# Layer 1 of a four-layer graph network: one 128-row product, or two 64-row products in two PSUM banks

## The chip, the cores and the metric

The kernel runs on one core of a Trainium2 chip. The time is device microseconds of one execution; for the kernel before it is the median of three runs. The profile is of one more execution, taken by the hardware profiler. The engines are PE (TensorE; PEld is its weight load), DVE (VectorE), ACT (ScalarE), POOL (GpSimd) and SP (SyncE, which issues DMAs). PSUM is the memory that PE writes its products to, in banks of 512 float32 columns on 128 partitions.

## The reference

A graph has 6250 nodes with 128 features and 206250 edges, sorted by destination. Four layers follow each other. Each normalises `x`, takes the part above zero as `h`, gathers `h` over the edges and adds its output to `x`:

```python
edge_index = jnp.stack([src, dst])
h = jnp.maximum(_layernorm(x), 0.0)
x = x + layer0(h, edge_weight, src, dst)   # weighted sums over edges, two linear maps, leaky relu
h = jnp.maximum(_layernorm(x), 0.0)
x = x + layer1(h, edge_index)              # mean over edges, see below
h = jnp.maximum(_layernorm(x), 0.0)
x = x + layer2(h, x_clique, edge_index)    # mean of x_clique rows over edges, one linear map
h = jnp.maximum(_layernorm(x), 0.0)
x = x + layer3(h, edge_index)              # sums over edges, a gated unit, one linear map

def layer1(x, edge_index):
    src, dst = edge_index
    deg = segment_sum(ones, dst, num_segments=n)
    agg = segment_sum(x[src], dst, num_segments=n) / jnp.maximum(deg, 1.0)[:, None]
    f = gelu(agg @ Wl.T + bl + x @ Wr.T, approximate=False)
    ...                                    # normalised over all nodes, plus x
```

## The kernel before

The nodes lie in 49 blocks of 128. The first part (function `strip`, lines L620 to L916) goes over 25 strips of two blocks of destination nodes. It turns the edges into one-hot matrices, and products of 64 rows each (`count`, L754) make from them, for a strip, a matrix of edge counts and one of edge weights, source by destination. Layer 0 runs in the same part: `layer0` (L791) multiplies `h0` with the weights matrix `edge_w` of the strip before, in float32. A float32 product takes two instructions on PE. Each block of 128 source nodes is taken there as two products of 64 rows, into two banks of the tile `pL`; ACT copies one bank (L796) and DVE adds the other (L797). `finish0` follows with full-height products of 128 rows (L825, L826, L846) and 64-row transposes (L809). The counts are written to DRAM (`cnt_d`) as one byte each.

Layers 1 to 3 then use the counts as a dense matrix. The function `dense` (L935) goes over 13 chunks of destination nodes, in `CHUNKS`: 11 of four blocks (512 columns), one of three (384) and one of two (256). For a chunk it accumulates, over all 49 blocks of source nodes, into one PSUM tile `acc` of two buffers. The features are held as two parts whose sum is `h` (`parts`, type fp32r), so each source block needs two products, j = 0 and 1: 98 products per chunk, 1274 per layer. This is L992. The right-hand side is a block of the counts, widened from bytes to fp32r.

A chunk is cut into 10 steps of up to five source blocks. For a step, `bring` fetches the bytes by DMA from SP's queue (tile `ring`, one fetch for two steps) and widens them into one of three buffers `wide`: in layer 1, where `seen` is given and each widening also counts the edges, three or two blocks by DVE (L973) and two or three by ACT (L975). `bring` for step n + 1 stands in the program ahead of the products of step n. All of this is under a hand-written schedule (`manual_schedule`): each engine executes its instructions in the order of the program text.

Work behind a chunk is a generator, `end1` for layer 1. `run` calls it when the chunk's last products have been issued. Its first piece, `copied` (L1114), brings the sum from `acc` to the SBUF tile `wa` with an ACT copy (L1116). Its later pieces run one by one between the steps that follow (`between`): `times` (L1123, four full-height float32 products with the weights `wl`), the scaling on DVE (L1131), the gelu on ACT (L1137), sums over nodes on POOL (L1020), and a subtraction (L1145). Also put between the steps of layer 1 are products for the inverse degrees (L1075), for a first mean (L1029) and for the last clique row (L1156). `end2` and `end3` use `copied` too.

[...] `pB` and `pM` are used by `end2` and `end3` (L1233, L1237, L1254, L1265), not by `end1`.

Of the kernel before, what the change touches and what calls it, by code (L numbers as in the profile page):

```python
# [9 lines left out]
F32 = mybir.dt.float32  # L10
# [6 lines left out]
P = 128  # L17
# [457 lines left out]
CB = 4  # L475
# [23 lines left out]
def fast(ctx: ExitStack, tc: tile.TileContext, a: dict, out: bass.AP, flag: bass.AP):  # L499


    nc = tc.nc
# [47 lines left out]
    def flat(t):  # L550
        return t.rearrange("p b f -> p (b f)")
# [47 lines left out]
    with ExitStack() as bx:  # L599
# [6 lines left out]
        psum = bx.enter_context(tc.tile_pool(name="b_psum", bufs=1, space=bass.MemoryType.PSUM))  # L606
# [304 lines left out]
        end = ends.pop()  # L911
# [21 lines left out]
    psum = ctx.enter_context(tc.tile_pool(name="f_psum", bufs=1, space=bass.MemoryType.PSUM))  # L933

    def dense(parts, by_node, seen=None, ahead=None):  # L935


        last = NB if by_node else NQB
        held = []

        def bring(c, g, nb, q):

            now = wide.tile([P, KP, CB * P], F32R, name="wide")
            if not by_node:
                t = ring.tile([P, KQ, CB // 2 * P], U16, name="ring")
                n = -(-nb // 2) * P
                nc.sync.dma_start(t[:, :, :n], cntT_d[:, q : q + KQ, g // 2 * P : g // 2 * P + n])
                t = flat(t).bitcast(U8).rearrange("p (k r n e) -> p k r e n", k=KQ, n=P, e=2)
                for eng, k in ((nc.vector.tensor_copy, slice(0, 3)), (nc.scalar.copy, slice(3, 5))):
                    if nb == 1:  # L950
                        eng(now[:, k, :P], t[:, k, 0, 0])
                    else:
                        eng(now[:, k, : 2 * n].rearrange("p k (r e n) -> p e k r n", e=2, n=P),  # L953
                            t[:, k, : n // P].rearrange("p k r e n -> p e k r n"))
                return [(q + k, now[:, k, : nb * P]) for k in range(KQ)]
            e = q % 2
            if e == 0:
                if ahead and c == 0:
                    ahead(q + 2 * KP)
                t = ring.tile([P, CB, KP * P], U16, name="ring")  # L960
                nc.sync.dma_start(t[:, :nb], cnt_d[c, :, :nb, q // 2 * P : (q // 2 + KP) * P])
                held[:] = [flat(t).bitcast(U8).rearrange("p (b k n e) -> p e k b n", b=CB, k=KP, e=2)[:, :, :, :nb]]
            to = now[:, :, : nb * P].rearrange("p k (b n) -> p k b n", n=P)
            of = held[0][:, e]
            ks = min(KP, (NB - q + 1) // 2)
            if seen is None:
                nc.vector.tensor_copy(*(v[:, :3].rearrange("p k b n -> p b k n") for v in (to, of)))  # L967
                nc.scalar.copy(to[:, 3:ks], of[:, 3:ks])  # L968
            for k in range(ks if seen is not None else 0):
                s = q + 2 * k  # L970
                total = seen[:, c, s : s + 1]
                if k < 3 - e:
                    nc.vector.tensor_scalar(to[:, k], of[:, k], 1.0, None, op0=ALU.mult, op1=ALU.add, accum_out=total)  # L973
                else:
                    nc.scalar.activation(to[:, k], of[:, k], AF.Copy, accum_out=total)  # L975
            return [(q + 2 * k, now[:, k, : nb * P]) for k in range(ks)]

        chunks = [(c, *CHUNKS[c]) for c in ORDER] if by_node else [(c, *at) for c, at in enumerate(CHUNKS2)]
        end = NB - 2 if by_node else NQB - 1
        parts_of = [q + e for q in range(0, NB, 2 * KP) for e in range(2)] if by_node else range(0, NQB, KQ)  # L980
        steps = [(c, g, nb, q) for c, g, nb in chunks for q in parts_of]
        ready = bring(*steps[0])
        yield
        for n, (c, g, nb, q) in enumerate(steps):
            now = ready
            if n + 1 < len(steps):
                ready = bring(*steps[n + 1])
            if q == 0:
                acc = psum.tile([P, CB * P], F32, name="acc", bufs=2)
            for s, rhs in now:  # L990
                for j in range(2):
                    nc.tensor.matmul(acc[:, : nb * P], parts[:, s, j, :], rhs,  # L992
                                     start=s + j == 0, stop=s == end and j == 1)
            yield (g, nb, acc) if q == parts_of[-1] else None

    running, waiting = [], []
# [116 lines left out]

    def copied(acc, w):  # L1114
        agg = work.tile([P, CB * P], F32, name="wa", bufs=5)
        nc.scalar.copy(agg[:, :w], acc[:, :w])  # L1116
        return agg

    def times(agg, weight, nb):
# [6 lines left out]
    def end1(g, nb, acc):  # L1126
        agg = copied(acc, nb * P)
        yield
        pa = times(agg, wl, nb)
        for j in range(nb):  # L1130
            nc.vector.scalar_tensor_tensor(f[:, g + j, :], pa[:, j * D : (j + 1) * D],  # L1131
                                           inv1[:, g + j : g + j + 1], f[:, g + j, :],
                                           op0=ALU.mult, op1=ALU.add)
        yield
        fb = f[:, g : g + nb, :]
        fg = flat(fb)
        nc.scalar.activation(fg, fg, AF.Gelu)  # L1137
        over_nodes(f_sum, fb, g, nb)
        yield
        if g == 0:  # L1140
            yield
            p = over_all(fb, nb)
            nc.vector.scalar_tensor_tensor(first, p, 1.0 / (nb * P), mean_scale, op0=ALU.mult, op1=ALU.mult)
            yield
        nc.vector.tensor_sub(fb, fb, bcast(first, nb))  # L1145
        yield
        sq = work.tile([P, GB, D], F32, name="wb", bufs=3)
        nc.scalar.activation(sq[:, :nb, :], fb, AF.Square)
        over_nodes(sq_sum, sq, g, nb)
# [44 lines left out]
    def end2(g, nb, acc):  # L1194
        w = nb * P
        cols = slice(g * P, g * P + w)
        agg = copied(acc, w)
        yield
        pa = times(agg, wc, nb)
# [47 lines left out]
    def end3(g, nb, acc):  # L1247
        w = nb * P
        cols = slice(g * P, g * P + w)
        agg = copied(acc, w)  # L1250
        yield
        gates, r_z = [], ("pA", "pM")
# [41 lines left out]
    with tc.manual_schedule():  # L1294
# [18 lines left out]
        chores[11 * n1].append(lambda: nc.vector.tensor_add(b_rz, b_ih[:, :2], b_hh[:, :2]))  # L1313
        chores[11 * n1 + 3].append(lambda: nc.vector.tensor_add(b_res, gn_bias, bc))
        run(dense(h_parts, True, deg2, h_up_to), end1, chores)
        running.extend(waiting)
        running.append(graph_norm())
        waiting.clear()

        layer2 = dense(q_parts, False)  # L1320
        next(layer2)
        normed = running[-1]
        for done in layer2:
            between(normed not in running)
            if done:
                work_2 = end2(*done)
                next(work_2)
                waiting.append(work_2)
        layer3 = dense(m_parts, True)
        next(layer3)  # L1330

# [67 lines left out]
```

## Time and profile before

| what | value |
| --- | --- |
| median of three runs | 1887.61 us (1885.89 to 1888.15) |
| profiled execution, its own time | 1886.66 us |
| its span, first to last instruction | 1884.5 us |
| granted PE clock, mean | 0.988 |
| PE busy | 1783.6 us, 95% |
| DVE busy | 1397.3 us, 74% |
| ACT busy | 1204.7 us, 64% |
| POOL busy | 463.1 us, 25% |
| DMA, mean | 123 GB/s |

Layer 0 and the counting take the span up to about 1028 us, layer 1 from there to 1327, layer 2 to about 1507 and layer 3 the rest.

In the lines of the profile, a group has line, engine, operation, output<-inputs, shape and count, then busy time and the mean ns of one instruction, then the idle time of the engine ahead of it and what ended it. In a shape such as `64*128 64x256`, the first pair is the rows and columns of PE's array that a product takes, and the second the rows and columns that are streamed. A row of a timeline has the start, the length from the first start to the last end, and the number of like instructions that were merged into it. The profile marks fp32r products as f32. Ends of products are modelled; starts are recorded.

### The profile page before, as it was taken

To read this page: it belongs to the slowest core of one execution; us is meant where nothing else is said; L and a number is where in the kernel's file an instruction comes from. 1 tells how busy PE (TensorE), PEld (TensorE's weight loads), DVE (VectorE), ACT (ScalarE), POOL (GpSimd) and SP (SyncE) were. 2 spreads that over 40 slices of the span, in tenths; PEclk is the share of its full clock that TensorE was granted. 3 is DMA by queue.
4 is the path that set the end of the run, shared out by engine and by line. 5 is a ranking of instruction groups with operands and counts; after the bars stand their busy time and mean duration, and the time that the engine had idled before them with its cause. 6 is when DMAs were issued, how large, how long until landed. Compare 5 with 4: busy or idle time off the path is not lost. (4 is left out here: it accounts for less than half of the span.)

```text
span 1884.5 us, 65347 instructions
## 1 busy us (share of the span) xinstructions
PE 1783.6 (95%) x28188; PEld 1504.1 (80%) x28188; DVE 1397.3 (74%) x2952; ACT 1204.7 (64%) x2834; POOL 463.1 (25%) x429
## 2 busy tenths in 40 slices
PE   0799999999999999999997999999999999999997
PEld 0688888888888888888886788888888877787775
DVE  5888888888888888888873877777787845444543
ACT  2877777777777777777772677777565654444442
POOL 3224333433334323433321111111132200000000
PEclk9799999999999999999998999999999999999998
DMA  3235555554645554554212555554554544344431
GB/s 76 80 89 130 116 131 114 122 125 115 122 101 135 106 130 109 118 123 112 71 58 95 180 178 163 167 158 124 148 151 142 159 128 139 119 143 133 148 116 52
DMA packets 262350, 231.98 MB, mean 123 GB/s; under 512 B 101553, under 2 KB 246052, under 8 KB 262052
## 3 DMA queue, kind: packets, MB, share of 16 engines
q1 hardware_dynamic: 252243, 210.20, 41.4%
q0 software_dynamic: 8944, 17.12, 3.2%
q8 instruction: 223, 3.65, 0.8%
q10 hardware_dynamic: 864, 0.39, 0.2%
q14 instruction: 76, 0.61, 0.1%
HBM read 130.50 MB, written 76.67 MB: 110 GB/s over the span
## 5 line engine op out<-in xcount | busy, mean ns | idle before, releaser
L791 PE MATMUL pL<-edge_w,h 64*128 64x256 f32 (+1 forms) x4900 | 616.5, 386 | 5.0 <-DVE agg L797 1.0
L992 PE MATMUL acc<-wide,parts 128*128 128x512 f32 (+2 forms) x2548 | 578.8, 386 | 12.8 <-DVE wide L973 9.4
L992 PEld LDWEIGHTS acc<-wide,parts 128*128 128x128 f32 x2548 | 463.9, 190 | 112.8 <-issue 14.5
L763 ACT CAST cnt<-pK 128x400 uint8<-128x400 f32 x784 | 396.6, 506 | 197.8 <-PE pK L754 181.7
L791 PEld LDWEIGHTS pL<-edge_w,h 64*128 64x128 f32 x4900 | 433.9, 187 | 46.3 <-DVE agg L797 6.7
L754 PEld LDWEIGHTS <-s_hot 64*128 64x128 bf16 x18816 | 371.7, 95 | 69.9 <-issue 18.5
L754 PE MATMUL pK<-k_hot,s_hot 64*128 64x49 bf16 (+1 forms) x18816 | 389.0, 193 | 21.6 <-ACT edge_w L761 11.9
L761 ACT COPY edge_w<-pK 128x392 f32<-128x392 f32 x784 | 399.5, 510 | 0.0
L735 DVE TENSOR_TENSOR k_hot<-k_hot,by_edge 128x2352 bf16<-128x2352 bf16 x196 | 272.8, 1392 | 8.0
L732 DVE TENSOR_TENSOR s_hot<-iota,keys 128x2048 bf16<-128x2048 bf16 x196 | 240.0, 1224 | 41.2 <-PE pK L754 37.9
L973 DVE TENSOR_SCALAR_CACHE_REDUCE wide<-ring 128x512 fp32r<-128x512 uint8 (+2 forms) x325 | 193.2, 650 | 27.6 <-issue 15.3
L975 ACT ACTIVATE wide<-ring 128x512 fp32r<-128x512 uint8 (+2 forms) x312 | 184.8, 595 | 38.9 <-ACT wide L975 19.9
L642 POOL DMA_INDIRECT dst<-in_dst,off_i x50 | 83.4, 1668 | 401.2 <-DVE node L680 394.4
L968 ACT CAST wide<-ring 128x1024 fp32r<-128x1024 uint8 (+3 forms) x130 | 120.8, 957 | 77.0 <-PE acc L992 66.7
L967 DVE CAST wide<-ring 128x1536 fp32r<-128x1536 uint8 (+2 forms) x130 | 118.9, 938 | 58.6 <-PE acc L992 41.5
L992 PE MATMUL acc<-wide,q_parts 128*128 128x512 f32 (+2 forms) x650 | 157.4, 392 | 1.2 <-DVE wide L953 1.2
L992 PEld LDWEIGHTS acc<-wide,q_parts 128*128 128x128 f32 x650 | 115.7, 189 | 28.1 <-DVE wide L953 3.1
L734 DVE TENSOR_TENSOR k_hot<-iota,keys 128x800 bf16<-128x800 bf16 x196 | 126.4, 645 | 0.0
L1288 POOL DMA_DIRECT2D out<-x x12 | 10.0, 837 | 320.9 <-DVE x L1286 290.9
L1267 DVE SCALAR_TENSOR_TENSOR wb<-pT,f_b_hh,wb 128x512 f32<-128x512 f32 (+2 forms) x13 | 9.4, 720 | 97.2 <-PE pT L1264 90.7
L642 POOL DMA_INDIRECT src<-in_src,off_i x50 | 76.4, 1527 | 15.2 <-issue 14.6
L1116 ACT COPY wa<-acc 128x512 f32<-128x512 f32 (+2 forms) x39 | 21.8, 560 | 82.6 <-PE acc L992 82.6
(181 smaller groups left out, 1564.6 us busy)
## 6 DMA issues: line engine op xcount, KB each, us to landing
ring<-cnt_d SPq DMA_DIRECT2D x110, 640.0 KB, 4.4
cnt_d<-cnt SPq DMA_DIRECT2D x49, 800.0 KB, 4.1
cntT_d<-tt SPq DMA_DIRECT2D x125, 160.0 KB, 2.0
ring<-cntT_d SPq DMA_DIRECT2D x60, 320.0 KB, 3.2
ring<-cnt_d SPq DMA_DIRECT2D x10, 480.0 KB, 3.7
ring<-cnt_d SPq DMA_DIRECT2D x10, 320.0 KB, 3.0
xs<-in_x SPq DMA_DIRECT2D x12, 256.0 KB, 3.0
xs<-in_x SPq DMA_DIRECT2D x24, 128.0 KB, 3.8
```

Source lines behind the costliest of these rows:

```text
L642: nc.gpsimd.indirect_dma_start(out=t, out_offset=None, in_=col[name], in_offset=bass.IndirectOffsetOnAxis(ap=idx, axis=0))
L732: nc.vector.tensor_tensor(s_hot, count_up(P), at(0, P), op=ALU.is_equal)
L734: nc.vector.tensor_tensor(k_hot[:, :, 0], count_up(NBP), at(1, NBP), op=ALU.is_equal)
L735: nc.vector.tensor_tensor(k_hot[:, :, 1:, :NB], k_hot[:, :, :1, :NB].to_broadcast([P, tq, 3, NB, TI]), parts.to_broadcast([P, tq, 3, NB, T ...
L754: nc.tensor.matmul(pk[:, h, to], s_hot[r, u, :, t], rhs, start=j == 0, stop=True, skip_group_check=True)
L761: nc.scalar.copy(m.rearrange("p b (i h) -> p b i h", h=WN), by_block[:, 1, :NB])
L763: nc.scalar.copy(m.rearrange("p b e (i h) -> p b e i h", h=WN), by_block[:, 0].rearrange("p (b e) i h -> p b e i h", e=2))
L791: nc.tensor.matmul(pl[:, h, :w], h0[r, s, :], edge_w[r, s, :w], start=s == 0, stop=s == NB - 1)
L968: nc.scalar.copy(to[:, 3:ks], of[:, 3:ks])
L973: nc.vector.tensor_scalar(to[:, k], of[:, k], 1.0, None, op0=ALU.mult, op1=ALU.add, accum_out=total)
L975: nc.scalar.activation(to[:, k], of[:, k], AF.Copy, accum_out=total)
L992: nc.tensor.matmul(acc[:, : nb * P], parts[:, s, j, :], rhs, start=s + j == 0, stop=s == end and j == 1)
```

## The change

In layer 1 alone (`seen` is given there and nowhere else), a chunk gets a second PSUM tile of 512 columns, `pB` and `pM` in turn. Each product of 128 source nodes becomes two: the first 64 nodes into `acc`, the last 64 into the second tile, one directly behind the other. `copied` copies the first tile with ACT as before, and DVE then adds the second one to the copy. In layers 2 and 3 `acc` is a list of one tile, and the products are those of before.

```diff
             if q == 0:
-                acc = psum.tile([P, CB * P], F32, name="acc", bufs=2)
+                acc = [psum.tile([P, CB * P], F32, name="acc", bufs=2)]
+                if seen is not None:
+                    acc.append(psum.tile([P, CB * P], F32, name=("pB", "pM")[n // len(parts_of) % 2]))
             for s, rhs in now:
                 for j in range(2):
-                    nc.tensor.matmul(acc[:, : nb * P], parts[:, s, j, :], rhs,
-                                     start=s + j == 0, stop=s == end and j == 1)
+                    for i, t in enumerate(acc):
+                        r = slice(i * P // len(acc), (i + 1) * P // len(acc))
+                        nc.tensor.matmul(t[:, : nb * P], parts[r, s, j, :], rhs[r],
+                                         start=s + j == 0, stop=s == end and j == 1)
             yield (g, nb, acc) if q == parts_of[-1] else None
...
     def copied(acc, w):
         agg = work.tile([P, CB * P], F32, name="wa", bufs=5)
-        nc.scalar.copy(agg[:, :w], acc[:, :w])
+        nc.scalar.copy(agg[:, :w], acc[0][:, :w])
+        if len(acc) > 1:
+            nc.vector.tensor_add(agg[:, :w], agg[:, :w], acc[1][:, :w])
         return agg
```

## Prediction

> **What bounds the kernel now.** I read the page first. Its slices show the TensorE (PE) busy at nine tenths nearly throughout, and its groups put layers 1 and 3 (line L992, `parts`) at the largest cost but one:
>
> ```profile
> L791 PE MATMUL pL<-edge_w,h 64*128 64x256 f32 (+1 forms) x4900 | 616.5, 386 | 5.0 <-DVE agg L797 1.0
> L992 PE MATMUL acc<-wide,parts 128*128 128x512 f32 (+2 forms) x2548 | 578.8, 386 | 12.8 <-DVE wide L973 9.4
> ```
>
> L791 is layer 0, which already works in halves of 64 rows. Then I cut the span at the layers with the table by windows. Layer 1 runs from 1029 to 1327 us:
>
> ```profile
> 1028.00:1327.00 299.00, 292.22 (x1389) 244.51 (x1390) 225.71 (x737) 211.81 (x664) 50.07 (x55) 0.99 0.54 164
> 1100.00:1150.00 50.00, 50.00 (x230) 41.60 (x229) 37.83 (x121) 36.66 (x112) 9.26 (x9) 1.00 0.59 178
> ```
>
> The columns are length, then busy time of PE, its weight loads, DVE, ACT and POOL. Once the layer has started (from about 1053 us), PE has next to no idle time up to its last, narrow chunk. So what a product costs on PE goes straight into the time, and DVE (38 of 50 us) matters only where PE must wait for it.
>
> The PE timeline gives the pace; the first two rows are from a view of a whole chunk, the last two from views cut inside a chunk:
>
> ```profile
> 1113.63 1.05 PE L1123 MATMUL pA<-f_WlT,wa 128*128 128x128 f32 x8
> 1114.44 22.50 PE L992 MATMUL acc<-wide,parts 128*128 128x512 f32 x98
> ...
> 1119.78 10.59 PE L992 MATMUL acc<-wide,parts 128*128 128x512 f32 x46
> ...
> 1162.69 10.58 PE L992 MATMUL acc<-wide,parts 128*128 128x384 f32 x60
> ```
>
> A row runs from its first start to its last end. 46 products in 10.59 us, less one duration of 0.39, over 45 steps, make 0.227 us each; with 384 columns (10.58 - 0.34) / 59 = 0.1736. The 53 ns between them for 128 columns are 0.415 ns per column; 512 columns make 0.212, so 14 ns of the 227 depend on no column. Only these 14 ns can be saved by any arrangement that streams the same columns. The whole chunk's row, 22.50 - 0.39 over 97 steps, holds 0.09 more than 97 x 0.227: its first product takes longer.
>
> **The pairs.** The change replaces each of layer 1's 1274 products (98 steps in 13 chunks) by two with 64 rows each and all of its columns (512 in 1078 of them), into two banks. Work streamed per row of the array is the same; so nothing is gained unless part of the 14 ns goes. The trace shows such pairs in layer 0, from the PE timeline:
>
> ```profile
> 990.50 12.34 PE L791 MATMUL pL<-edge_w,h 64*128 64x256 f32 x112
> ...
> 1004.22 0.94 PE L791 MATMUL pL<-edge_w,h 64*128 64x128 f32 x12
> ...
> 1005.11 0.89 PE L791 MATMUL pL<-edge_w,h 64*128 64x128 f32 x12
> 1005.93 0.49 PE L825 MATMUL po<-f_W1T,agg 128*128 128x128 f32 x2
> 1006.25 0.39 PE L826 MATMUL po<-f_W2T,inter 128*128 128x128 f32 x2
> 1006.48 0.39 PE L825 MATMUL po<-f_W1T,agg 128*128 128x128 f32 x2
> 1006.70 0.39 PE L826 MATMUL po<-f_W2T,inter 128*128 128x128 f32 x2
> 1007.02 2.95 PE L791 MATMUL pL<-edge_w,h 64*128 64x128 f32 x48
> ```
>
> 112 products are 56 pairs, two starts some 0.01 apart: (12.34 - 0.38 - 0.01) / 55 = 0.217 us a pair with a longer first one in it, 0.216 without. One such product takes 0.377 by itself, so two in 0.216 do run at once, with two weight loads. Half against whole shows at 128 columns: 24 pairs in 2.95, less 0.27 for the last, 0.01 and 0.08 for the longer first, over 23, are 0.1126; eight full-height products in L1123's 1.05, less 0.275, over 7, are 0.111. So halves are 1 to 2 ns dearer than the whole in f32, and not cheaper. For layer 1's number type (fp32r, half the cycles per column) no 64-row pair is in this trace. Bounds: down to 0.216 (the f32 pair, which streams as long) saves 1274 x 11 ns = 14 us; both fixed parts in a row, 0.227 + 0.014 = 0.241, costs 18 us; no overlap at all, 2 x 0.227, costs 289 us. I take the nearest comparison, half against whole in one type: +1 ns, 1.3 us, with 0 to 2.5 as its range.
>
> [...]
>
> **Switching between halves and whole.** Lines L1123, L1075, L1029 and L1156 keep full-height products and are put between the steps. Before, that costs little: from the last L992 before L1123 to the first behind it is one product plus 0.81 us and 0.09 for the longer first one, against 8 x 0.111 = 0.89 of work. In layer 0 it costs more. From 1005.11 to 1007.02 are 1.91 us, with six pairs (6 x 0.113 = 0.68) and eight full products (0.89) in them: 0.34 are lost, and about 0.08 in the longer first pair behind it. L825's first row shows part of it: two products in 0.49, where the later rows take 0.39. That is 0.4 us there and back. In layer 1 stand 12 groups of L1123 and one each of L1075, L1029 and L1156: 15 x 0.4 = 6.0, and half of that, 0.2, at the step into layer 2. Sum 6.2; if only the visible gaps between the groups count and the weights are fetched ahead as now, some 3. I take 6.2, as the rows are of the same engine with the same weights' size.
>
> **The add on DVE.** Thirteen new adds on DVE (after the ACT copy L1116) take the second bank in. The price of one is that of L1286, also 512 columns with one operand in PSUM:
>
> ```profile
> L1286 DVE TENSOR_TENSOR x<-x,pA x13: 421/689/689, 1560.8 to 1876.9; 128x512 f32<-128x512 f32 x11, 128x384 f32<-128x384 f32 x1, 128x256 f32<-128x256 f32 x1
> ```
>
> 13 x 0.69 are 9 us of DVE, which has 73 us idle in the layer. The price is in the order: the add stands behind the widening of step n+1 and ahead of that of step n+2, so DVE, which now runs two steps ahead of PE, waits at the chunk's end for PE and ACT. One chunk's end, from the ACT timeline:
>
> ```profile
> 1132.44 0.59 ACT L1116 COPY wa<-acc 128x512 f32<-128x512 f32 x1 [2.69 <-PE acc L992]
> ```
>
> The last product's tail (0.39 - 0.227 = 0.16) and 0.03 of signal lie ahead of the copy, so PE began the next chunk at 1132.25. The copy ends at 1133.03, the add (0.03 later, as L797 follows L796) at 1133.75, and the first widened block of step n+2 is there at 1134.44 (L973 takes 0.69, and one follows another after 0.61). PE wants it 10 x 0.227 behind 1132.25, at 1134.52. It is hidden by 0.08, the second block, 0.61 later, is wanted 0.45 later and comes 0.07 late. With semaphores I put 0.1 to 0.2 on each of ten wide chunks, 0.5 where the next chunk has 384 columns and 0.7 where it has 256: 2.5 us. If the cover fails and each add counts whole, 9 us; if the ring of three `wide` buffers takes all, 0. L1123 comes 20 products after the copy, so it does not wait. Behind the add stand L1131 and the widening only; the halving of `h` is over by the second chunk. DMAs and queues are not moved. The banks `pB` and `pM` are unused in this layer, and a bank returns two chunks later.
>
> **Sum.** 1.3 + 6.2 + 2.5 = 10.0 us on the profiled execution's 1886.66 gives 1896.7. The median of the runs stands 0.95 above that execution: 1897.6. A change under 0.2% (3.8 us) can't be told from none here.
>
> **Rivals.** *Gain:* the fixed 14 ns belong to the full height, and 64-row pairs go at 0.216 as in L791: -14 + 6.2 + 2.5 = -5.3, so 1882.3 us, faster. It decides as soon as a pair saves 7 ns (8.7 / 1274). For it speaks that 227 exceeds 216 for the same streaming; against it, that f32 shows no difference between halves and whole. *Fixed parts in a row:* the pair takes 0.241; 18 + 8.7, about 1914. *No overlap:* fp32r halves wait for each other, and the change does not do what it says: 289 + 8.7, about 2185. For it speaks only that fp32r takes a column in half the time of f32 and no pair of it is shown; against it, that bf16 pairs (L754) run at that column rate, in short bursts.
>
> **How the numbers follow.** My forecast 60% (1889 to 1903 from the bounds of the three terms), gain 17%, fixed parts in a row or a pair in between 12%, no overlap 11%. The range from 1880 to 1916 holds the forecast, most of the gain and half of the third; it leaves out the last. Of the forecast's 60, 8 lie within 0.2% and 1 below; of the gain's 17, 1 lies within. Faster 17%, same 9%, slower 74%.
>
> **What would show it.** Behind the change a wide chunk's row in the PE timeline should have 196 products in about 22.6 us; 21.6 would show the gain, 24 the fixed parts in a row, 44 no overlap. Around L1123 the time from L992 to L992 should grow by 0.3 to 0.4 us. DVE should show 13 waits of its new add for ACT, some 2.5 us each, and PE short waits for `wide` about 2.3 us behind them. Layers 0, 2 and 3 should keep their lengths; if they don't, the sum is wrong whatever the total.

## The result, and the profile after

The changed kernel takes 1898.16 us (median of four runs, 1896.81 to 1899.44) against 1887.18 for the kernel before beside it: a ratio of 1.0059, interval 1.0041 to 1.0076. It is slower by 11 us, and the forecast was 10 us. The sum came out nearly right, but not all of its terms did: the pairs were too dear, the add too cheap, and an effect of the clock was missing.

Layer by layer, from the first product of each layer to the first of the next:

| us | before | after | second profile of before | second profile of after |
| --- | --- | --- | --- | --- |
| ahead of layer 1 | 1029.2 | 1030.1 | 1033.4 | 1033.7 |
| layer 1 | 297.3 | 307.4 | 297.6 | 307.3 |
| layer 2 | 186.0 | 186.8 | 185.4 | 186.7 |
| layer 3 to the end | 372.0 | 371.7 | 371.4 | 371.6 |

The last two columns are of one chip, from the runs `before_again` and `after_again` below. Layer 1 grows by 10.1 and 9.7. The stretch ahead of it scatters. Layer 2 grows by 0.8 and 1.3, which will turn out to be an effect of the clock.

The PE timeline of the changed kernel, first around a group of full-height products (L1129, the line that was L1123), then near a chunk's start. The two tiles of a pair alternate, so the view merges nothing:

```profile
1116.05 0.39 PE L996 MATMUL acc<-wide,parts 64*128 64x512 f32 x1
1116.05 0.39 PE L996 MATMUL pM<-wide,parts 64*128 64x512 f32 x1
1116.37 1.16 PE L1129 MATMUL pA<-f_WlT,wa 128*128 128x128 f32 x8
1117.46 0.49 PE L996 MATMUL acc<-wide,parts 64*128 64x512 f32 x1
...
1117.79 0.39 PE L996 MATMUL acc<-wide,parts 64*128 64x512 f32 x1
...
1135.72 0.39 PE L996 MATMUL acc<-wide,parts 64*128 64x512 f32 x1
...
1137.77 0.39 PE L996 MATMUL acc<-wide,parts 64*128 64x512 f32 x1
...
1138.04 0.50 PE L996 MATMUL acc<-wide,parts 64*128 64x512 f32 x1
```

Three things are to be seen. The two halves start together. The starts go on by 0.227 to 0.228 (nine steps from 1135.72 to 1137.77 are 2.05); over the 1063 steps of 512 columns that no other product interrupts, the median is 227 ns in both kernels. And around L1129 from 1116.05 to 1117.79 are 1.74 us, with two steps (0.45) and 0.89 of work in them: 0.40 lost, where the kernel before lost 0.01. Of it 0.09 is the later start of L1129 (0.32 after the pair), 0.11 its own longer first product (1.16 against 1.05), 0.09 the later start of the pair behind it (0.205 after the last product, against 0.111) and 0.11 that pair's longer length. The start at 1138.04, 0.27 after the last, is the first product of a step that waited for DVE.

The waits of layer 1 say who is late:

```profile
DVE wa L1122 <- ACT wa L1120: 33.9, 13, 3.5
...
DVE fh L1137 <- PE pA L1129: 17.4, 12, 1.5
...
PEld acc L996 <- DVE wide L973: 15.6, 36, 2.5
...
PE acc L996 <- DVE wide L953: 1.9, 1, 1.9
```

Columns are us in total, times, longest. DVE waits 2.6 us at each of 13 chunk ends before it may add (L1122), and PE's weight loads wait 36 times for `wide`, 15.6 us. Before it was 17 times and 10.9:

```profile
PEld acc L992 <- DVE wide L973: 10.9, 17, 2.3
```

L1137 (before L1131) waits 17.4 instead of 38.5: DVE has spent its lead at the add. The last row is new: at the step into layer 2, PE waits 1.9 us for the widening L953, and the DVE and PE timelines show why:

```profile
1336.12 0.42 DVE L1122 TENSOR_TENSOR wa<-wa,pB 128x256 f32<-128x256 f32 x1 [2.87 <-ACT wa L1120]
1336.46 1.82 DVE L953 CAST wide<-ring 128x1536 fp32r<-128x1536 uint8 x2
```

```profile
1337.56 4.13 PE L996 MATMUL acc<-wide,q_parts 128*128 128x512 f32 x10 [1.87 <-DVE wide L953]
```

L953 of layer 2 widens three blocks in one operation of 0.9 us. In the kernel before, the first two of these began at 1324.60 and 1326.12, ahead of the end of layer 1's last products. Now the add stands ahead of both, so nothing of them is there before 1337.4. And the first ten products of layer 2 take 4.13 us where the kernel before has 2.77: most of them start 0.43 apart, at a granted clock of 0.50 (from 1337.59 to 1341.00).

```profile
1326.50 2.77 PE L992 MATMUL acc<-wide,q_parts 128*128 128x512 f32 x10
```

### The profile page after: what moved, and what is told of

It reads as the page before. It is cut to its first block, busy times and chain, and to the rows that moved or that the text cites. A ratio compares the mean times of both kernels' runs of the same rounds, so it can differ in the third digit from the quotient of the medians.

```text
span 1896.0 us, 67896 instructions
## 1 busy us (share of the span) xinstructions
PE 1792.4 (95%) x29462; PEld 1503.9 (79%) x29462; DVE 1402.5 (74%) x2965; ACT 1204.8 (64%) x2834; POOL 460.7 (24%) x429
## 5 line engine op out<-in xcount | busy, mean ns | idle before, releaser
L996 PE MATMUL acc<-wide,parts 64*128 64x512 f32 (+5 forms) x2548 | 580.0, 384 | 13.2 <-DVE wide L973 9.6
L996 PEld LDWEIGHTS acc<-wide,parts 64*128 64x128 f32 (+1 forms) x2548 | 457.5, 187 | 118.3 <-DVE wide L973 15.6
L973 DVE TENSOR_SCALAR_CACHE_REDUCE wide<-ring 128x512 fp32r<-128x512 uint8 (+2 forms) x325 | 192.5, 649 | 19.1 <-ACT wide L975 12.1
L996 PE MATMUL pB<-wide,parts 64*128 64x512 f32 (+1 forms) x686 | 154.6, 379 | 0.0
L996 PE MATMUL pM<-wide,parts 64*128 64x512 f32 (+1 forms) x588 | 132.5, 380 | 0.0
L996 PEld LDWEIGHTS pB<-wide,parts 64*128 64x128 f32 x686 | 119.6, 186 | 0.0
L996 PEld LDWEIGHTS pM<-wide,parts 64*128 64x128 f32 x588 | 105.8, 184 | 0.0
```

The source lines that it names most:

```text
L996: nc.tensor.matmul(t[:, : nb * P], parts[r, s, j, :], rhs[r], start=s + j == 0, stop=s == end and j == 1)
```

## The experiments

All comparisons of times are with the kernel before on the same chip, run beside; lengths of layer 1 are held against the 297.3 and 297.6 of the two profiles of the kernel before. The theory: a switch between halves and whole costs 0.39 us there and back, 5.9 in layer 1; the add's place on DVE costs 4, of which 2 at the step into layer 2; the pairs cost nothing.

**The add later.** `copied` keeps only the ACT copy; the add goes into `end1`'s next piece.

```diff
         agg = copied(acc, nb * P)
         yield
+        nc.vector.tensor_add(agg[:, : nb * P], agg[:, : nb * P], acc[1][:, : nb * P])
         pa = times(agg, wl, nb)
```

> The halves stay, and the add of the second bank moves on DVE from the end of the chunk to just ahead of the products L1123, two steps later. Theory (switches cost about 6 us, the add's place on DVE about 4, the pairs nothing): layer 1 loses its waits behind the chunk's end and the 1.9 us at the step into layer 2, and stands 6 us over before, about 1893.5 in all. Rival (the add's place costs nothing, and PE's extra waits come from the halves themselves): no change against the changed kernel, about 1898.

Measured: 1894.77 against 1890.05, ratio 1.0022 (1.0013 to 1.0032). Layer 1 takes 302.4, some 5 us less than the changed kernel and 4.7 to 5.1 over before. The step into layer 2 is back to 0.2 us. On DVE the add no longer waits:

```profile
1116.24 0.68 DVE L1133 TENSOR_TENSOR wa<-wa,pB 128x512 f32<-128x512 f32 x1
1119.93 1.13 DVE L1136 SCALAR_TENSOR_TENSOR fh<-pA,inv,fh 128x128 f32<-128x128 f32 x4 [3.01 <-PE pA L1127]
```

So the same add costs nothing when it stands where DVE has its lead already. What is left is near the 5.9 of the switches, a little under it. Step by step against the kernel before, the 15 places with whole products, with the pair behind each, are 5.8 us longer than in its first profile, and all other steps together 0.7 us shorter.

**The add alone.** Whole products, and a read of `acc` by DVE in the place of the add.

```diff
         agg = copied(acc, nb * P)
+        nc.vector.tensor_max(agg[:, : nb * P], agg[:, : nb * P], acc[:, : nb * P])
         yield
```

> The products stay whole, and in layer 1 DVE reads acc (a maximum of the copy and acc, which is the copy) in the place where the change adds the second bank. Theory: it costs what the add's place costs, about 4 us, of which nearly 2 at the step into layer 2: about 1891. Rival: under 1 us, 1887 to 1888.

Measured: 1895.70 against 1890.05, ratio 1.0031 (1.0019 to 1.0042). Layer 1 takes 302.3, 4.6 to 4.9 over before, and nothing else in the kernel is changed. About 2.0 of it lie at the step into layer 2, the rest, 2.6 to 2.9, at chunk starts. The two parts alone add up: 4.7 to 5.1 for the switches and 4.6 to 4.9 for the add make 9.3 to 10.0, where the two together take 9.7 to 10.1. Theory held; its 4 were too small by 0.6 to 0.9.

**More switches.** The four products of L1123 in two places, two by two, with the same work:

```diff
-        pa = times(agg, wl, nb)
-        for j in range(nb):
-            nc.vector.scalar_tensor_tensor(f[:, g + j, :], pa[:, j * D : (j + 1) * D], ...)
-        yield
+        pa = psum.tile([P, CB * D], F32, name="pA", bufs=2)
+        for part in (range(2), range(2, nb)):
+            for j in part:
+                nc.tensor.matmul(pa[:, s], agg[:, s], wl, start=True, stop=True)
+            for j in part:
+                nc.vector.scalar_tensor_tensor(f[:, g + j, :], pa[:, j * D : (j + 1) * D], ...)
+            yield
```

> The changed kernel with the four products of L1123 put in two places, two behind one step and two behind the next. This makes 12 more switches there and back in layer 1 and no more work on PE. Theory (0.39 us each): about 4.7 us over the changed kernel, 1902.5 to 1903. Rival (what an insertion loses is paid by the products' weights and not by the switch, or is hidden elsewhere): within 1.5 us of the changed kernel.

> The same split in the kernel before, where all products are whole. Theory: 12 insertions without a switch cost 0.01 to 0.02 us each, under 0.5 us: 1887 to 1888. Rival (a split costs by itself, by its products or by DVE's smaller pieces): as much as in the halves, 4 to 5 us.

Measured: with halves 1904.98 against 1890.05, ratio 1.0077 (1.0060 to 1.0094); layer 1 takes 312.5, 5.1 over the changed kernel, which is 0.43 for each of 12, near the 4.7 expected. With whole products 1889.17, ratio 0.9995 (0.9986 to 1.0005); layer 1 takes 296.4, 1 us less than before. The same edit costs 5 us in one kernel and nothing in the other: what an insertion loses is the switch.

**No switch at L1123.** With the add later, L1123's products of the 12 wide chunks in halves too, into the two buffers of `pA`, with eight operations on DVE behind them in place of four.

```diff
-        pa = times(agg, wl, nb)
-        for j in range(nb):
-            nc.vector.scalar_tensor_tensor(f[:, g + j, :], pa[:, j * D : (j + 1) * D], ...)
+        both = [psum.tile([P, CB * D], F32, name="pA", bufs=2) for _ in range(2)]
+        for j in range(nb):
+            for i, pa in enumerate(both):
+                r = slice(i * H, (i + 1) * H)
+                nc.tensor.matmul(pa[:, s], agg[r, s], wl[r], start=True, stop=True)
+        for pa in both:
+            for j in range(nb):
+                nc.vector.scalar_tensor_tensor(f[:, g + j, :], pa[:, j * D : (j + 1) * D], ...)
```

> The add stands two steps later as in the run before, and the products L1123 of the 12 wide chunks are taken in halves of 64 rows too, into the two buffers of pA, with four more operations of 0.28 us on DVE for each chunk. 12 of 15 switches are gone. Theory: 12 x 0.39 = 4.7 us under the kernel that has only the add later, so about 1 to 2 us over before, 1888.5 to 1890. It can't be faster than before, as a pair takes as long as a whole product. Rival (the longer gaps around L1123 are not the switch): no faster than with the add later alone.

Measured: 1941.00 against 1928.66 on a slower chip (its layer 1 begins 41 us later), ratio 1.0057 (1.0039 to 1.0075). That is a miss: 11 us over before by the ratio and 12 by the medians, not 1 to 2. The switch at L1140 did go, as the next run's lines show, but DVE's row behind L1140 grew:

```profile
1158.57 2.16 DVE L1145 SCALAR_TENSOR_TENSOR fh<-pA,inv,fh 128x128 f32<-128x128 f32 x8 [2.81 <-PE pA L1140]
```

In the kernel before, this row takes 1.13 us; DVE returns to widening one microsecond later, and PE's waits for L973 rise to 23.9 us at the weight loads, from 10.0 with the add later alone. The second bank must be added somewhere, and here it cost more than the switches.

**The same, with DVE's eight operations in two steps.** The second bank's four come one step later:

```diff
-        for pa in both:
+        for i, pa in enumerate(both):
+            if i:
+                yield
             for j in range(nb):
```

> As the run with L1123 in halves, but DVE takes the second bank's four operations one step later than the first bank's, so that it is as late as before when it goes back to widening. Theory (the 11 us over before in that run are DVE's eight operations in a row, not PE's pairs): the waits of PE for wide shrink to those of before, layer 1 takes about 298 to 300 us, 1 to 3 us over before. Rival (12 more pairs of banks or the halves of L1123 cost PE itself): 8 to 11 us over before, as in that run.

Measured: 1892.77 against 1889.12, ratio 1.0018 (1.0008 to 1.0027). Layer 1 takes 300.5, 2.9 over the second profile of before, at the upper end of the 1 to 3 expected. The PE timeline around the group:

```profile
1116.94 0.39 PE L996 MATMUL acc<-wide,parts 64*128 64x512 f32 x1
...
1117.17 1.05 PE L1140 MATMUL pA<-f_WlT,wa 64*128 64x128 f32 x16
1117.98 0.47 PE L996 MATMUL acc<-wide,parts 64*128 64x512 f32 x1
```

Sixteen halves take the 1.05 us of the eight whole products, and the next pair follows 0.81 after their start, just as in the kernel before. So with all in halves PE has no loss and no gain at this place; three switches (1.2 us) and waits for `wide` are left. Neither place tried for the second bank made the halves faster than the whole.

**One half alone.** The second halves and the add are not there.

```diff
+                        if t is None:
+                            continue
                         r = slice(i * P // len(acc), (i + 1) * P // len(acc))
```

> Layer 1's second halves are left out (64 of each 128 source nodes are not summed), and the add with them. One 64-row product at a time. Theory (the part of the 227 ns that depends on no column belongs to the number type and not to the height): a step stays at 227 ns. Rival (a pair hides something that a single product shows, or the other way): below 220 or above 235.

Measured: 2181.6 us, one run. A step takes 427 ns, which is above 235, but for a reason that neither expectation has. The table by windows inside layer 1, and a row of the PE timeline there:

```profile
1100.00:1200.00 100.00, 100.00 (x244) 76.19 (x243) 45.58 (x141) 38.49 (x111) 7.99 (x8) 0.50 0.30 88
```

```profile
1239.38 21.11 PE L998 MATMUL acc<-wide,parts 64*128 64x512 f32 x49
```

The column behind the engines is the granted PE clock: 0.50, with PE busy all the time. A product takes (21.11 - 0.61) / 48 = 0.427, nearly twice the time of before. The clock had fallen to 0.50 at 1068.5, in the waits ahead of layer 1 (its mean from 1050 to 1100 is 0.68), and it came back only at 1624.9, some 4 us into layer 2's whole products. So the run can't tell what the 227 ns are made of at full clock. At half clock half and whole cost the same: the changed kernel's whole products at the start of layer 2 also start 0.43 apart.

**Another number type.** What would make a product of 512 columns cheaper, then? The kernel before, in one line:

```diff
-F32R = mybir.dt.float32r
+F32R = mybir.dt.bfloat16
```

> The kernel before with whole products, and fp32r replaced by bf16 in the widened counts and in both parts of the features, in layers 1 to 3 (the sum of the parts is then coarser). Theory (14 ns fixed belong to fp32r, bf16 has about 3, as L709 with 128 columns follows itself after 56 ns): a product of 512 columns takes 216 ns, 11 ns less for each of 3198, 35 us where PE is the bound: about 1855. Rival (the fixed part comes from loading new weights for each product, whatever the type): 227 ns, no change.

> The kernel with bf16 in place of fp32r once more, on another chip if there is one: 35 us under before, a ratio of 0.981.

Measured: 1893.47 against 1928.66, ratio 0.9809 (0.9793 to 0.9826), and on the other chip 1853.96 against 1889.12, ratio 0.9807 (0.9788 to 0.9826): 35 us faster than before, as expected. It beats both kernels. The second run's PE timeline inside a chunk:

```profile
1121.72 10.52 PE L992 MATMUL acc<-wide,parts 128*128 128x512 bf16 x48
```

(10.52 - 0.38) / 47 = 0.216 us a product, against 0.227. The 11 ns that the rival *Gain* hoped to get from the height of the tile belong to the number type. Layer 1 takes 284.2, where it was 297. The features' two parts are kept in bf16 then; how much coarser that makes their sum is not told by the times.

**The two kernels once more.**

> The kernel before, unchanged, for a second profile beside the next one. Layer 1 297 us, layer 2 186, layer 3 372; what differs from the first profile by more is the profile's own scatter.

> The changed kernel, unchanged, on the same chip as the run before it. Layer 1 307 us, 10 over the other; the start of layer 1 and layers 2 and 3 should agree within 1 us if the 1.0 us ahead of layer 1 and the 0.8 in layer 2 of the first two profiles were scatter.

Measured: 1890.07 and 1901.12. The table at the top has their layers. Layer 1 agrees with the first profiles, and the start of layer 1 scatters by more than its first difference. Layer 2, however, is over again, by 1.3. The run with the add alone has the same wait at the step into layer 2, and this row:

```profile
1336.81 2.56 PE L992 MATMUL acc<-wide,q_parts 128*128 128x512 f32 x10 [1.88 <-DVE wide L953]
```

Ten products in 2.56 us after 1.88 of idle time: the clock held, at 1.00 from 1335 to 1342. In both profiles of the changed kernel it was lower behind the wait: 0.50 from 1337.59 to 1341.00 in the first, 0.57 in the mean from 1341 to 1345 in the second. That looks as if halves ahead of a wait brought the clock down, but the table by windows has a fall with whole products too. Here are stretches of 3.41 us, two of the changed kernel, one of the run with the add alone, and two from layer 1 of the kernel before in its second profile (behind the window stand its length and PE's busy time, third from the end the granted clock):

```profile
1334.18:1337.59 3.41, 1.54 (x27) 1.36 (x23) 1.47 (x3) 1.88 (x3) 0.00 (x0) 1.00 0.37 103
1337.59:1341.00 3.41, 3.41 (x8) 2.73 (x9) 0.69 (x1) 1.33 (x2) 0.00 (x0) 0.50 0.69 180
...
1335.25:1338.66 3.41, 1.85 (x8) 1.57 (x9) 2.16 (x3) 2.93 (x4) 0.00 (x0) 1.00 0.20 38
...
1040.21:1043.62 3.41, 1.43 (x5) 0.81 (x6) 3.21 (x9) 1.51 (x6) 0.54 (x1) 1.00 0.84 271
1043.62:1047.03 3.41, 3.41 (x9) 2.63 (x9) 2.79 (x8) 0.78 (x3) 0.54 (x1) 0.50 0.73 233
```

In the changed kernel PE has no work for 1.87 us of the first stretch, and the clock is 0.50 in the next. With the add alone it has none for 1.56 us of the stretch, as 0.32 of the wait lie ahead of it, and the clock stays at 1.00. In the kernel before, with whole products, PE has none for 1.98 us of one stretch, and the clock is 0.50 in the next. So the clock fell without halves too, and that they have a part in it is not shown; nor is why it held with the add alone. In the changed kernel the wait of 1.9 us was followed by products at half the clock, and layer 2 took another 0.8 to 1.3 us.

## Why the prediction was right, by its steps

- **The pairs** (+1.3): 0.0. They run at once, and a pair costs what the whole costs, 0.227. The rivals *No overlap*, *Fixed parts in a row* and *Gain* fall with that. The argument for *Gain*, 227 against 216 for the same streaming, compared two number types. The argument against it, half against whole in one type, was the one that held.
- **The switches** (6.2): 0.39 to 0.40 at each L1129 in the trace, 5.8 to 5.9 for all 15. The half switch at the step into layer 2 can't be told from the wait that stands there. The cost was read off layer 0's L825 and held for another number type. The run with more switches gave 0.43 each, the add-later run 4.7 to 5.1 in all.
- **The add on DVE** (2.5): mis-sized, 4.2 in the changed kernel (10.1 in layer 1, less 5.9 for the switches) and 4.6 to 4.9 alone. The chunk starts were right: 2.2 by the first sum, 2.6 to 2.9 with the add alone. The failing step is that of 13 adds only 12 were priced, and the step into layer 2 was charged with half a switch alone. I had followed the add's queue for 512, 384 and 256 columns in layer 1, but not for the last chunk, behind which stands layer 2's L953 with three blocks in one operation: 2.0 us. "Behind the add stand L1131 and the widening only" overlooks it.
- **The clock** was in no term: 0.8 to 1.3 us in layer 2. The prediction itself said that layer 2 should keep its length and that the sum is wrong if it doesn't.
- **The sum** (10.0 on 1886.66; 1897.6 with the runs' median): 11.1 between the two profiled executions and 11.0 between the medians. Pairs 1.3 too dear, switches 0.3 too dear, the add 1.7 too cheap, the clock about 1 missed. That the total is within a microsecond is partly luck. The stated 1889 to 1903 doesn't follow from the bounds of the three terms: 0 to 2.5, 3 to 6.2 and 0 to 9 on 1887.6 give 1890.6 to 1905.3. The result lies in both.
- **The sign to look for**: a row of 196 products can't be had, as alternating tiles aren't merged. From one L1129 to the next (1116.37 to 1140.08) are 23.71 us against 23.15, 0.40 of the 0.56 for the switch.

## What to carry to other kernels

Splitting a product that already fills the array's height gained nothing here: each half streams all columns, and a pair took the 0.227 us of the whole. Compare half and whole in the same number type before hoping for the difference between two types. Count how often whole and split products alternate, as each change there and back cost 0.4 us here. An operation that waits belongs where its engine has no lead to lose: the same add cost 4.6 to 4.9 us at the chunk's end and caused no wait two steps later, and what stands behind it at the border to the next stage has to be followed too.

## What the runs showed that was not expected

- With 64-row products one at a time and no pause, a granted clock that had fallen to 0.50 ahead of layer 1 stayed there for all of the layer's 545 us (427 ns between starts of 512 columns), with PE 100% busy. In the changed kernel layer 1 begins at 0.50 too, and pairs of them had the clock back at 1.00 after 3.7 us (1030.14 to 1033.80). Why is open, and so is whether single ones would lose the full clock.
- At the step into layer 2, PE's wait of 1.87 us in the changed kernel was followed by 3.41 us at a granted clock of 0.50, and layer 2 took 0.8 to 1.3 us more. A wait of 1.88 us with the add alone was followed by 1.00. Why is open.
- fp32r costs 11 ns more than bf16 for each whole product of 512 columns, 0.227 against 0.216, at the full clock.
